# A third nested Strassen product in the attention projection, with its plain products read by ScalarE and added by GpSimd

## The chip, the cores and the metric

The kernel runs on one core of one Trainium2 chip. A core has five engines that run side by side: TensorE (PE in the profile, with its weight loads as PEld), VectorE (DVE), ScalarE (ACT), GpSimd (POOL) and SyncE (SP), which issues most of the DMAs here. The metric is the device time of one execution in microseconds (us), the median of several.

## The reference, cut to what matters

Eight images of 512 channels and 32x32 positions (1024) go through two layers. The first is self-attention with 8 heads of 64 channels:

```python
q = conv1x1(x, Wq, bq); k = conv1x1(x, Wk, bk); v = conv1x1(x, Wv, bv)   # all 512 x 512
attn = softmax(einsum('bhdn,bhdm->bhnm', q, k) * scale, axis=-1)
out = einsum('bhnm,bhdm->bhdn', attn, v)
x = x + conv1x1(out, Wp, bp)
```

The second is a non-local block: theta, phi and g are 1x1 convolutions of this x to 256 channels, f is theta times phi transposed over 1024, y is f times g, a further 1x1 convolution brings y back to 512 channels and adds x, and a batch normalisation over all images ends it. All of it is float32.

## The kernel before, in words

The images are worked off one after the other (the loop over `b`). For each image the order on TensorE is: attention of image b; q, v and k of image b+1; the projection Wp times the attention's output o of image b, called **p** (tiles `pp` and `pp_in`); theta and phi in one product (`ptp`); g (`pg`); f, wf and z. TensorE's instructions are pinned to the order in which the program gives them (`pe`), and so are all instructions marked `dve` or `sp` on the engine they run on; others may be placed by the tile framework where its own model finds the engine free. The framework makes all semaphores, and hands out buffers: a tile of a tag waits until the last reader of the tile that held that buffer is done.

**Products.** A matrix product is split into quarters 11, 12, 21 and 22 and done by Strassen's scheme in Winograd's form: seven products of sums of quarters (`SEVEN`), whose results are added up in several quarters of the output. A product's name is 11, s1t1, s2t2, s4, s3t3, 12 or t4; `s1` to `s4` are sums of weight quarters (blocks 3 to 6 of `Weights`), `t1` to `t4` sums of data quarters (`more_sums`). Each entry gives the product's name, its weight block, its data, its PSUM slot, and the quarters that it is read into, with a mark where the reading is the first (and then adds the bias).

**Nested products.** A product may itself be done by seven smaller ones (`nested`). That needs four inner sums of its weights (`inner_weights`), kept beside the block, and four of its data (`inner_sums`). For p of images 1 to 6, `FIVE` plain products (11, s1t1, s2t2, s4, s3t3) stand beside two nested ones, weight block 1 with data 21 and block 2 with t4. `INNER` holds this, and a list of counts: how many nested steps follow each plain matmul of the program. A matmul of the program is two instructions in the profile[...]. Image 0 and the last image use seven plain products.

**Slots.** PSUM is four tags of two banks each; `free` is the order in which they are to be taken. `seven` takes tags[0] and tags[1] for the slots 0 and 1 of its plain products and, with nested products, tags[2] and tags[3] for these. A later product in the same slot accumulates on what lies there, after it has been read. At its start it sets the order for the next stage, with nested products so:

```python
free[:] = [tags[1], tags[2], tags[3], tags[0]]
```

In p, slot 0 holds 11, s2t2 and s3t3 in turn, slot 1 s1t1 and s4. Theta/phi (`theta_phi`) is again a `seven` with nested products, and starts from this order.

**Reading p.** `project` reads each product from PSUM on VectorE into xt, the image's x in SBUF (line 782 with the bias, line 477 without). xt is then theta's data; its sums t1 and t2 (line 267) are made on VectorE, t4 and the inner sums of t4 and 21 on GpSimd, by `sums`, called after theta's first product.

**GpSimd's queue around p.** During v, GpSimd multiplies o by the reciprocal sums and adds v's parts. After the first third of k come the inner sums of quarter 21 of o (line 279), t1 to t4 of o (line 267) and the inner sums of t4; then `six` has it add up k: 12 += 22, 12 += T6 in its middle, 22 += T7, 21 += T7 at its end (line 402). T6 and T7 are scratch tiles of the pool `w3` (tag "acc", three buffers), which also holds theta's bias `tpb`, g and the attention's sums `acc`. Blocks of 128x1024 (`block`) come from a ring of twelve.

**Weights.** They are loaded per image, in up to three units, into four buffers (`wr`) by SP, as buffers come free (`load_w`, `fetch`); for Wp the units are blocks (1, 2), (3, 4, 5) and (6). A unit of two blocks is "roomy": it has room for inner sums. In image 0 the sums are made and the units stored in DRAM (`keep`, `keep_two`).

Of the kernel before, what the change touches and what calls it, by code (L numbers as in the profile page):

```python
# [30 lines left out]
def unshifted(ctx: ExitStack, tc: tile.TileContext, a: dict, out: bass.AP):  # L31
# [79 lines left out]
    for b in range(1, B):  # L111
# [2 lines left out]
    loaded, ahead = [], {"unit": [], "first": []}  # L114

    PAIRS = ((1, 6), (3, 4), (5, 2))
    UNITS = {"WqT": PAIRS, "WkT": PAIRS, "WvT": PAIRS, "WpT": ((1, 2), (3, 4, 5), (6,)), "tp": ((1, 2), (3, 4, 5), (6,)),
             "WgT": (range(7),)}
    WIDTH = 14 * P

# [39 lines left out]
    def fetch(w, n, t=None, dma=None):  # L160
        dma, name = dma or nc.sync, w.name
        if t is None:
            t = wf0.tile([P, 2 * w.half], F32, tag="w0", name=f"w0_{name}") if n == "first" else \
                wr.tile([P, WIDTH], F32, tag="w", name=f"w_{name}_{n}")
        blocks = w.place(n, t)
        if name in kept:
            of = kept["plain" if w.last else name][n]
            sp(dma.dma_start(w.whole(n) if w.last else w.tiles[n], of))
            return
        if n == 0:  # L170
            corner[name] = block(f"a21_{name}")[:, :, :w.half]
            sp(dma.dma_start(corner[name], quarter(name, 1, 0)))
        for i, m, k in ((0, 0, 0), (1, 0, 1), (2, 1, 1)):
            if i in blocks:
                sp(dma.dma_start(w[i], quarter(name, m, k)))
# [32 lines left out]
    def inner_weights(w, i):  # L208

        a11, a12, a22, a21, s2, s3, s4 = w.inner(i)  # L210
        return [lambda to=to, l=l, r=r, op=op: dve(nc.vector.tensor_tensor(to, l, r, op))
                for to, l, r, op in ((s3, a11, a21, ALU.subtract), (a21, a21, a22, ALU.add), (s2, a21, a11, ALU.subtract),
                                     (s4, a12, s2, ALU.subtract))]

    def nest(w, i):
        for one in inner_weights(w, i):
# [65 lines left out]
    def quarters_of(t):  # L282
# [16 lines left out]

    INNER = {"p": (FIVE, ((1, "21", "11", False), (2, "t4", "21", True)), [0] * 4 + [1] * 14),
             "tp": (FIVE, ((2, "t4", "21", True), (1, "21", "11", False)), [0] * 24 + [1] * 14)}

    def nested(name, w, data, tags, first, add, goes_to, positions_out):
# [25 lines left out]
                yield  # L331

    def seven(name, w, data, positions_out, first, add, between=None, early=False,
              by_chunk=False, inner=None):

        nk, half = w.shape[2], w.shape[3]
        tags = list(free)
        free[:] = [tags[3], tags[1], tags[0], tags[2]] if early else [tags[3], tags[1], tags[2], tags[0]]  # L340
        slots, begun = {}, set()
        steps, counts = iter(()), iter(())
        if inner:
            free[:] = [tags[1], tags[2], tags[3], tags[0]]
            products, goes_to, counts = INNER[inner]
            counts = iter(counts)
            steps = nested(name, w, data, tags[2:], first, add, goes_to, positions_out)
        else:
            products = LATER if early == "later" else EARLY if early else SEVEN

        def read(reads, ps):
            for to, is_first in reads:
                (first if is_first else add)(to, ps)

        for n, (what, wi, di, s, reads) in enumerate(products):
            if s not in slots or early and what == "t4":
                slots[s] = bank(tags[s], f"{name}_{s}_{n}")
                begun -= {one for one in begun if one[0] == s}
            ps, d = slots[s], data[di]
            if positions_out:  # L360
                parts = [(ps.rearrange("p h (i f) -> p (h i) f", f=half)[:, i, :], i * half // 512,
                          lambda k, i=i: d[:, k, i * P:(i + 1) * P], lambda k: w[:, wi, k, :])
                         for i in range(512 // P)]
            else:
                parts = [(ps[:, m, :], m, lambda k, m=m: w[:, wi, k, m * P:(m + 1) * P], lambda k: d[:, k, :])
                         for m in range(half // P)]
            work = [(*part, k) for part in parts for k in range(nk)]
            if by_chunk and what in ("11", "s1t1"):
                work.sort(key=lambda one: one[4])
            for i, (to_ps, at, lhsT, rhs, k) in enumerate(work):  # L370
                pe(nc.tensor.matmul(to_ps, lhsT(k), rhs(k), start=(s, at) not in begun, stop=(k == nk - 1),  # L371
                                    skip_group_check=True))
                begun.add((s, at))
                for _ in range(next(counts, 0)):
                    next(steps)
            read(reads, ps)
            if between and n in between:
                between[n]()

    SIX = (((1, "21", "11"), (6, "22", "12")), ((3, "t1", "22"), (4, "t2", "T6")), ((5, "t3", "T7"), (2, "t4", "21")))  # L380
    ORDER = "0a 0b 1a 2a 2b 1b 5a 4a 5b 4b 3a 3b 6a 6b".split()

    def six(name, w, data, positions_out, at, begin, third, fills, by_scalar=False):

        fills = dict(fills)
        shape = [P, 4, 256] if positions_out else [P, 2, 512]
# [75 lines left out]
        assert not fills, fills  # L462
        if by_scalar:
            add("T7", "T6")
        add("22", "T7")
        add("21", "T7")

    def rows(q):
        return q[0] if isinstance(q[0], slice) else slice((int(q[0]) - 1) * CC // 2, int(q[0]) * CC // 2)
# [65 lines left out]
    def heads_of(b, what, w, bias, data, pin=lambda ins: None, steps=None, fills=None, **how):  # L535

        t = mats.tile([P, CC, N], F32, tag=what, name=f"{what}_{b}")

        if fills is not None:
            def begin(to, ps, i):  # L540
                nc.scalar.activation(to, ps, AF.Identity, bias=bias[:, i:i + 1])

            def third(to, ps, of, i):
                if what == "q":
                    nc.scalar.activation(to, ps, AF.Identity, bias=steps[:, i:i + 1])
                else:
                    dve(nc.vector.scalar_tensor_tensor(to, ps, steps[:, i:i + 1], of, ALU.add, ALU.add))

            six(f"p{what}_{b}", w, data, False, lambda q: t[:, rows(q), cols(q)], begin, third, fills,
                what == "q")  # L550
            return t

        def first(q, ps):
            for m in range(2):
                c = rows(q).start + m
                if how.get("early") and q == "21":
                    nc.vector.tensor_scalar(t[:, c, cols(q)], ps[:, m, :], bias[:, c:c + 1], 1.0, ALU.add, ALU.mult)
                else:
                    nc.scalar.activation(t[:, c, cols(q)], ps[:, m, :], AF.Identity, bias=bias[:, c:c + 1])

        seven(f"p{what}_{b}", w, data, False, first, add_to(t, pin), **how)

        return t
# [208 lines left out]
            return o["o"], lambda ps: denominators(1, ps), lambda d: normalize((first_den, d))  # L772
        return o["o"], all_denominators, normalize

    def project(b, xt, w, between, data):
        def first(q, ps):
            if isinstance(q[0], slice):
                ps = ps.unsqueeze(1)
            for m in range(ps.shape[1]):
                c = rows(q).start + m  # L780
                at = xt[:, c, cols(q)]
                ins = nc.vector.scalar_tensor_tensor(at, ps[:, m, :], bp[:, c:c + 1], at, ALU.add, ALU.add)  # L782
                if b == B - 1 and q in ("11", "22"):
                    dve(ins)

        seven(f"pp_{b}", w, data, False, first, add_to(xt), between, early=b == B - 1 and "later",
              inner="p" if 0 < b < B - 1 else None)

# [8 lines left out]
    def theta_phi(b, w, data, tpb, between):  # L799
# [26 lines left out]
        def sums():  # L826
# [3 lines left out]
            if b:  # L830
                for of in ("t4", "21"):
                    inner_sums(data, of, dve, nc.gpsimd)

        def third_sum():
            if "t3" not in data:
# [227 lines left out]
    for b in range(B):  # L1063
        last = b == B - 1
        nxt = {}
        if b == 1:
            nest(w_tp, 1)
            nest(w_tp, 2)
            keep("tp", w_tp, (0,))
# [40 lines left out]
        if not last:  # L1110
# [13 lines left out]
            o_sums = [lambda i=i: more_sums(nxt["o"], (i,), dve, nc.gpsimd) for i in range(1, 5)]  # L1124
            if b:
                more = [lambda: inner_sums(nxt["o"], "t4", dve, nc.gpsimd)]
                o_sums = [lambda: inner_sums(nxt["o"], "21", dve, nc.gpsimd), *o_sums]
            else:
                w_p = loaded[1]
                more = [lambda i=i: weight_sums(w_p, corner["WpT"], (i,), dve, nc.gpsimd) for i in (3, 4, 5)]  # L1130
            k = heads_of(b + 1, "k", weights("WkT"), bk, data, dve, steps=dk, fills={
                (0, 13): [*o_sums, *(more if b else ())], (1, 13): () if b else more,
                (2, 0): () if b else [lambda: dve(nc.vector.tensor_tensor(bp, bp, got, ALU.add)),
                                      lambda: weight_sums(w_p, corner["WpT"], (6,), dve, nc.gpsimd)]})
        else:
            nonlocal_(b - 1, held["x"], nxt["data"], held["f"], weights("WgT"), lambda: None,
                      {4: lambda: nxt.update(d=denominators(next_bank(f"den_{b}_1")[:, 0, :]))})
# [13 lines left out]
        if not last:  # L1151
            tpb = load_tpb(b)
        w = weights("WpT", sums_done=True)
        project(b, xt, w, between, nxt["o"])
        if b == 0:
            w_p = w
        load_w("first")
# [4 lines left out]
        if b == B - LATE:  # L1162
            for cc in range(CC):
                nc.sync.dma_start(spill[b][:, cc, :], xt[:, cc, :])
        data = data_sums(quarters_of(xt), f"x1_{b}", (1, 2, 3, 4) if last else (1, 2))
        of_theta = []
        w = weights("tp")
        between = {4 if b else 5: lambda: of_theta.append(f_sums(b, tps[0], 0))}
# [268 lines left out]
```

## Time and profile before

| | us |
|---|---|
| median of 3 runs | 2102.09 (2101.91 to 2103.84) |
| the profiled execution | 2103.74 |
| its span, first to last instruction | 2102.0 |
| TensorE busy in it | 2078.5 |
| VectorE, ScalarE, GpSimd busy | 1442.3, 788.6, 734.0 |
| p of image 1, from its first weight load to theta's | 23.21 |

The span is what lies between the first and the last instruction of the profiled execution; the time of that execution is 1.7 us longer. One image is 257 us. A busy share over the whole span mixes stages: in attention VectorE and ScalarE are loaded most, around p they are not. The profile names, for idle time of an engine, the instruction that ended it. "xN" behind a row of the timeline says that N like instructions are merged in it; a row's length is that of all of them.

### The profile page before, as it was taken

The page shows a single profiled execution, that of the slowest core. Times are in us where ns is not written, and L with a number is a line of the kernel's source. Part 1 is how long each engine was busy: PE and PEld are TensorE (multiplying, and loading weights), DVE is VectorE, ACT ScalarE, POOL GpSimd, SP SyncE. Part 2 cuts the span into 40 slices and gives each one's busy share as a digit, 9 for nine tenths or more (in the row PEclk, how much of TensorE's full clock was granted, in tenths as well). Part 3 has the DMA queues.
Part 4 walks back from the last instruction along what each step waited for, and adds up shares of the span by engine and source line. Part 5 has one row for each costly group of instructions (what it writes and reads, how often), then busy time and mean ns, then how long its engine had stood idle before and what let it go on. Part 6 is the DMA issues. An engine that isn't in the chain of part 4 may idle for free.

```text
span 2102.0 us, 34269 instructions
## 1 busy us (share of the span) xinstructions
PE 2078.5 (99%) x13646; PEld 1170.3 (56%) x13646; DVE 1442.3 (69%) x2169; ACT 788.6 (38%) x1043; POOL 734.0 (35%) x637
## 2 busy tenths in 40 slices
PE   9999999999999999999999999999999999999995
PEld 4535864358733677336773377633776348743472
DVE  5587567875677656776567766677665775676756
ACT  1465203652046410464105641066312653056106
POOL 0024800348113581134812356123660338411010
PEclk9999999999999999999999999999999999999998
DMA  6254534345343443435324363253644345212668
GB/s 230 83 144 78 162 137 143 42 83 157 105 115 38 89 148 106 119 39 114 132 92 122 40 142 122 69 126 40 155 149 154 39 48 174 99 30 40 218 253 321
DMA packets 77263, 246.80 MB, mean 117 GB/s; under 512 B 17188, under 2 KB 25640, under 8 KB 75048
## 3 DMA queue, kind: packets, MB, share of 16 engines
q1 hardware_dynamic: 63224, 218.17, 31.8%
q0 software_dynamic: 12016, 24.80, 12.2%
q8 instruction: 110, 1.80, 0.4%
q10 hardware_dynamic: 1856, 1.56, 0.3%
q14 instruction: 57, 0.47, 0.1%
HBM read 163.20 MB, written 47.71 MB: 100 GB/s over the span
## 4 chain that ended last, share of the span: by engine, by line
PE 98%; ACT 1%; DVE 1%; DMA 0%; issue 0%; DVEq 0%
PE ps L611 21%; PE po L637 21%; PE pp L371 7%; PE ptp L371 7%; PE pv_in L447 6%; PE pq_in L450 6%; PE pk_in L450 6%; PE pg L371 5%; PE pz L371 3%; PE pf L866 2%; PE ptp_in_s L319 2%; PE pp_in_s L322 2%; PE pwf L909 1%; PE pv L414 1%; PE pq L417 1%; PE pq L371 1%
## 5 line engine op out<-in xcount | busy, mean ns | idle before, releaser
L614 ACT ACTIVATE e<-ps 128x1024 f32<-128x1024 f32 x512 | 522.4, 1024 | 428.7 <-PE ps L611 418.0
L667 POOL DMA_DIRECT2D fold<-acc x336 | 257.2, 816 | 949.2 <-DMA fold<-acc 450.4
L620 DVE TENSOR_TENSOR acc<-acc,e 128x1024 f32<-128x1024 f32 x384 | 469.9, 1224 | 94.5 <-ACT e L614 84.6
L611 PE MATMUL ps<-q,k 64*64 64x512 f32 x4096 | 529.3, 589 | 0.0
L637 PE MATMUL po<-e,v 64*64 64x512 f32 x4096 | 528.8, 589 | 0.0
L637 PEld LDWEIGHTS po<-e,v 64*64 64x64 f32 x4096 | 156.7, 133 | 282.8 <-issue 275.5
L611 PEld LDWEIGHTS ps<-q,k 64*64 64x64 f32 x4096 | 155.6, 133 | 283.1 <-issue 274.9
L897 ACT ACTIVATE g<-pg,gb 128x512 f32<-128x512 f32 x31 | 21.3, 687 | 447.7 <-PE pg L371 447.6
L618 DVE TENSOR_TENSOR acc<-e,e 128x1024 f32<-128x1024 f32 x64 | 78.3, 1224 | 117.6 <-ACT e L614 115.4
L371 PE MATMUL pp<-t_o,w_WpT 128*128 128x512 f32 x208 | 101.0, 592 | 0.0
L371 PE MATMUL ptp<-w_tp,t_x 128*128 128x256 f32 x400 | 96.1, 379 | 0.0
L729 POOL TENSOR_TENSOR o<-o,r 128x1024 f32<-128x1024 f32 x28 | 65.5, 2359 | 36.0 <-DMA r<-den_d 35.5
L371 PEld LDWEIGHTS ptp<-w_tp,t_x 128*128 128x128 f32 x400 | 72.3, 190 | 7.8
L458 DVE TENSOR_TENSOR k<-k,pk_in 128x256 f32<-128x256 f32 x112 | 46.8, 421 | 39.4 <-PE pk_in L450 35.0
L371 PE MATMUL ptp<-w_tp,x 128*128 128x256 f32 x272 | 69.6, 380 | 0.0
L371 PE MATMUL pp<-o,w_WpT 128*128 128x512 f32 x144 | 67.7, 592 | 0.0
L456 ACT COPY v<-pv_in 128x256 f32<-128x256 f32 x84 | 31.4, 374 | 95.8 <-DVE T_pv L458 25.5
L458 DVE TENSOR_TENSOR v<-v,pv_in 128x256 f32<-128x256 f32 x112 | 46.2, 421 | 29.3 <-PE pv_in L447 22.8
L456 ACT COPY k<-pk_in 128x256 f32<-128x256 f32 x84 | 31.2, 372 | 93.3 <-PE pk_in L450 91.6
L782 DVE SCALAR_TENSOR_TENSOR x<-pp,bp,x 128x512 f32<-128x512 f32 x52 | 37.5, 746 | 33.0 <-PE pp L371 33.0
L447 PE MATMUL pv_in<-w_WvT,i_t_x 128*128 128x128 f32 x448 | 59.2, 275 | 0.0
L450 PE MATMUL pk_in<-i_t_x,w_WkT 128*128 128x256 f32 x224 | 58.1, 381 | 0.1
(246 smaller groups left out, 3166.0 us busy)
## 6 DMA issues: line engine op xcount, KB each, us to landing
fold<-acc POOLq DMA_DIRECT2D x336, 64.0 KB, 3.0
w_WqT<-kept_WqT SPq DMA_DIRECT2D x21, 896.0 KB, 5.9
w_WvT<-kept_WvT SPq DMA_DIRECT2D x21, 896.0 KB, 5.5
w_WkT<-kept_WkT SPq DMA_DIRECT2D x21, 896.0 KB, 6.7
r<-den_d SPq DMA_DIRECT2D x32, 512.0 KB, 7.7
x<-in_x_dram SPq DMA_DIRECT2D x30, 512.0 KB, 6.0
spill<-x SPq DMA_DIRECT2D x24, 512.0 KB, 4.3
z<-spill SPq DMA_DIRECT2D x24, 512.0 KB, 8.1
```

Source lines behind the costliest of these rows:

```text
L371: pe(nc.tensor.matmul(to_ps, lhsT(k), rhs(k), start=(s, at) not in begun, stop=(k == nk - 1), skip_group_check=True))
L447: pe(nc.tensor.matmul(ps[:, i, :], d[:, i * P:(i + 1) * P], a, start=start and not i, stop=True, skip_group_check=True))
L450: pe(nc.tensor.matmul(ps, a, d, start=start, stop=True, skip_group_check=True))
L456: nc.scalar.copy(piece(q, i, j), ps)
L458: dve(nc.vector.tensor_tensor(piece(q, i, j), piece(q, i, j), ps, ALU.add))
L611: pe(nc.tensor.matmul(ps[c * P // 2:(c + 1) * P // 2, j, :], k[r, p, keys], q[r, p, h * 512:(h + 1) * 512], start=True, stop=True, skip_gr ...
L614: nc.scalar.activation(e, ps, AF.Exp, scale=SCALE)
L618: nc.vector.tensor_tensor(accs[u], es[u, 0], e, ALU.add)
L620: ins = nc.vector.tensor_tensor(accs[u], accs[u], e, ALU.add)
L637: pe(nc.tensor.matmul(ps[j * D:(j + 1) * D, r, :], v[keys, m, (2 * p + j) * D:(2 * p + j + 1) * D], e[keys, j, :], start=(m == 0), stop=(m ...
L667: nc.gpsimd.dma_start(to, of, accum_op=ALU.add)
L729: dve((engine or nc.vector).tensor_tensor(at, at, of, ALU.mult))
```

## The change

For p of images 1 to 6:

- The plain products are four (`FOUR`: 11, s1t1, s2t2, s3t3). s4, which is block 6 with data 22, becomes a third nested product, and is the first of the three: the order is block 6, block 2, block 1. A nested step follows each of the first ten plain matmuls, then 2, 1, and 2 after each of the last four.
- s3t3 stands in slot 1 and not in slot 0, in a new tile of that tag, which does not accumulate on s1t1.
- s1t1 and s2t2 are copied from PSUM by ScalarE into ring blocks (two copies of 128x512 each), and GpSimd adds the blocks to x: s1t1 into quarters 22 and 12, s2t2 into 12, 22 and, held back to the end, 21.
- s3t3 is read by VectorE at the end (`last_read`): first quarter 22 with the bias, then theta's data sums t1 and t2, then quarter 21, all pinned in this order.
- The inner sums of quarter 22 of o are added at the head of GpSimd's sums of o.
- k's last two additions (22 += T7, 21 += T7) are not made at k's end but behind GpSimd's sums for theta/phi.
- The units of Wp are (1, 2), (3, 4) and (5, 6). Block 6 with its inner sums is made once, at the start of image 1 (`nest_apart`: a load, four VectorE subtractions and a store), and loaded for each image by a DMA of its own behind block 5's.

In image 0, weight sums 5 and 6 of Wp are made on VectorE behind k, not on GpSimd within k.

```diff
-    UNITS = {... "WpT": ((1, 2), (3, 4, 5), (6,)), ...
+    UNITS = {... "WpT": ((1, 2), (3, 4), (5, 6)), ...
...
+            if n == 2 and name == "WpT" and not w.last:
+                sp(dma.dma_start(w[5], of[:, 0, :].rearrange("p (k f) -> p k f", k=2)))
+                sp(dma.dma_start(w.tiles[n][:, WIDTH // 2:], kept["block 6"]))
...
+    def nest_apart(w, n, i):
+        t = w3.tile([P, N], F32, tag="acc", name="apart")[:, :WIDTH // 2]
+        to = t[:, :2 * w.half]
+        sp(nc.sync.dma_start(to, kept["plain"][n][:, 1, :]))
+        w.at[i] = to.rearrange("p (k f) -> p k f", k=2)
+        w.extra[i] = t[:, 2 * w.half:].rearrange("p (i f) -> p i f", i=3)
+        nest(w, i)
+        kept[f"block {i}"] = dram.tile([P, WIDTH // 2], F32, tag=f"block{i}", name=f"block{i}")
+        sp(nc.sync.dma_start(kept[f"block {i}"], t))
...
-    INNER = {"p": (FIVE, ((1, "21", "11", False), (2, "t4", "21", True)), [0] * 4 + [1] * 14),
+    FOUR = (SEVEN[0], ("s1t1", 3, "t1", 1, (("22", False), ("12", False))),
+            ("s2t2", 4, "t2", 0, (("12", False), ("22", False), ("21", False))),
+            ("s3t3", 5, "t3", 1, (("22", True), ("21", False))))
+
+    INNER = {"p": (FOUR, ((6, "22", "12", True), (2, "t4", "21", True), (1, "21", "11", False)),
+                   [1] * 10 + [2, 1] + [2] * 4),
...
-            if s not in slots or early and what == "t4":
+            if s not in slots or early and what == "t4" or inner == "p" and what == "s3t3":
                 slots[s] = bank(tags[s], f"{name}_{s}_{n}")
...
-            read(reads, ps)
+            if inner and what in via:
+                via[what](reads, ps)
+            else:
+                read(reads, ps)
...
-        add("22", "T7")
-        add("21", "T7")
+        ends = [lambda q=q: add(q, "T7") for q in ("22", "21")]
+        if later is not None:
+            later += ends
+            return
+        for one in ends:
+            one()
...
+        held = []
+        def by_scalar(reads, ps):
+            t = block(f"read_{b}")
+            for m in range(2):
+                nc.scalar.copy(t[:, m, :], ps[:, m, :])
+            for n, (q, _) in enumerate(reads):
+                def one(at=xt[:, rows(q), cols(q)]):
+                    dve(nc.gpsimd.tensor_tensor(at, at, t, ALU.add))
+                if n < 2:
+                    one()
+                else:
+                    held.append(one)
+
+        def last_read(reads, ps):
+            held[0]()
+            first("22", ps)
+            more_sums(x1, (1, 2), dve)
+            add_to(xt, dve)("21", ps)
...
+            for one in data["later"]:
+                one()
...
+            nest_apart(Weights("WpT"), 2, 6)
             nest(w_tp, 1)
...
-                o_sums = [lambda: inner_sums(nxt["o"], "21", dve, nc.gpsimd), *o_sums]
+                o_sums = [*(lambda of=of: inner_sums(nxt["o"], of, dve, nc.gpsimd) for of in ("22", "21")), *o_sums]
...
+            if b == 0:
+                weight_sums(w_p, corner["WpT"], (5, 6), dve)
```

## The prediction

> **What bounds the kernel now.** First the page's busy shares and the chain of work that ended last: what holds the end?
>
> ```profile
> PE 2078.5 (99%) x13646; PEld 1170.3 (56%) x13646; DVE 1442.3 (69%) x2169; ACT 788.6 (38%) x1043; POOL 734.0 (35%) x637
> ...
> PE 98%; ACT 1%; DVE 1%; DMA 0%; issue 0%; DVEq 0%
> ```
>
> TensorE (PE) is the bound from end to end, and asked for its waits between 262 and 2050 us the profile names none. So a matmul taken out is gained in full, and a new PE wait is lost in full. Next, the p stage of image 1 in the table by stretches, from its first weight load to theta's; images 2 to 6 read 23.20 to 23.21 us too.
>
> ```profile
> core 0: us, PE busy (x) PEld busy (x) DVE busy (x) ACT busy (x) POOL busy (x), PEclk, DMA share, GB/s
> 514.17:537.38 23.21, 23.21 (x70) 13.11 (x69) 12.64 (x23) 0.37 (x1) 12.51 (x9) 1.00 0.29 99
> ```
>
> PE is full; ScalarE (ACT) is free, VectorE (DVE) and GpSimd (POOL) half busy. Third, the timeline where p hands over to theta/phi (columns: start, length, engine, line, operation, count, idle time before and its releaser):
>
> ```profile
> 533.07 1.22 DVE L477 TENSOR_TENSOR x<-x,pp 128x1024 f32<-128x1024 f32 x1 [0.44 <-PE pp L371]
> ...
> 534.53 1.22 DVE L267 TENSOR_TENSOR t_x<-x 128x1024 f32<-128x1024 f32 x1
> ...
> 535.88 1.88 PE L371 MATMUL pp<-t_o,w_WpT 128*128 128x512 f32 x4
> ...
> 537.59 3.62 PE L371 MATMUL ptp<-w_tp,x 128*128 128x256 f32 x16
> ...
> 537.79 2.35 DVE L477 TENSOR_TENSOR x<-x,pp 128x1024 f32<-128x1024 f32 x2 [1.23 <-PE pp L371]
> 540.06 1.22 DVE L267 TENSOR_TENSOR t_x<-x,t_x 128x1024 f32<-128x1024 f32 x1
> ```
>
> Theta's first matmul follows p's last without a gap although DVE reads p's last product (s3t3) until 540.1. It can: s3t3 lies in p's slot 0, while `seven` leaves `free` as [tags1, tags2, tags3, tags0], so theta's first product takes p's slot 1, whose last read (s4's, 533.07) is long over. This is the hinge of my forecast. Fourth, POOL's own timeline around p:
>
> ```profile
> 502.28 0.73 POOL L279 TENSOR_TENSOR i_o<-o 128x256 f32<-128x256 f32 x1
> ...
> 517.51 2.36 POOL L402 TENSOR_TENSOR k<-k 128x1024 f32<-128x1024 f32 x1
> 519.95 6.96 POOL L402 TENSOR_TENSOR k<-k,T_pk 128x1024 f32<-128x1024 f32 x3
> 541.42 2.35 POOL L267 TENSOR_TENSOR t_x<-x,t_x 128x1024 f32<-128x1024 f32 x1 [14.51 <-DVE t_x L267]
> ```
>
> It is solid to 526.9, then idle 14.5 us.
>
> [...] in image 0 an add of 128x4 took 2.30 us beside a POOL subtraction:
>
> ```profile
> 249.28 2.34 POOL L267 TENSOR_TENSOR t_o<-o,t_o 128x1024 f32<-128x1024 f32 x1
> ...
> 249.34 2.30 DVE L1133 TENSOR_TENSOR bp<-bp,bias 128x4 f32<-128x4 f32 x1
> ```
>
> [...] The stage tables show 1.00[...].
>
> **The change part by part** (images 1 to 6, times of image 1).
>
> *Products.* By the timeline a plain product is eight 128x512 instructions at 0.429 us (3.43 us), a nested block fourteen 128x256 ones at 0.216 (3.02). p was 5 plain and 2 nested: 17.16 + 6.05 = 23.21, as measured. It becomes 4 and 3: 13.73 + 9.07 = 22.80. Gain 0.41 us per image, 2.4 in all. First matmul at 514.38 as before, so theta could start at 537.18 instead of 537.59.
>
> *Reads moved to ACT and POOL.* Four ACT copies of 128x512 (0.58 us by ACT's copies of `po`) lie in ACT's idle time; nothing is queued behind them before `g` at 563. POOL gets four more small subtractions ("22" of o, 2.9 us) at its queue's head, so k's "12" adds end at 525.1 instead of 522.3; two k adds leave; five adds to x at 2.36 us come. s1t1 ends on PE about 524.4, its copies 525.1: x22 to 527.5, x12 to 529.9. s2t2 ends at 530.0, its copies 530.65: x12 to 533.1, x22 to 535.4, x21 to 537.75. The two nested banks are wanted at 515.2, no longer at 518.7; k's last reads leave them at 514.6 and 514.95. Data sums that p needs from POOL, shifted by 2.9, keep 1.7 us or more: t4 is ready at 517.5 for a block starting 524.3, its inner sums at 520.4.
>
> *The slot.* `FOUR` puts s3t3, now last, into slot 1, in a new tile of that tag. Theta's first product still takes p's slot 1. So it must wait until DVE has read s3t3: twice for quarter 22, and for quarter 21, which `last_read` pins behind both of theta's sums t1 and t2. DVE's chain: p's last nested matmul starts 536.97, lasts 0.38, the read adds 0.42: 537.8. Quarter 22's two halves (0.75 each) can come earlier, as x22 is ready at 535.4 and their matmuls by 536.5; they push the last nested reads to about 538.0. Before, too, such halves ran ahead of nested reads that stand earlier in the program (522.75 before 523.41). t1 needs x11 whole: 538.0. Then t1, t2 and quarter 21, 1.13 from start to start and 1.22 for the last: 541.5. A wait of 541.5 - 537.2 = **4.3 us**. If quarter 22 comes after the nested reads, 5.4. Below: were sums and reads to overlap better than rows in a queue do, 3.7. I take 4.3. Queued behind it on PE is everything, so it moves the end. Under the same cover lies a smaller new wait: nested block 1 is now last, so x11 is complete 0.5 us after theta wants it.
>
> *k's last adds.* Two times 2.36 us, behind POOL's t4, inner t4 and inner 21: with the stall 541.5 to 549.7, then to 554.4. k's lower half is read half an attention later; T7's buffer is wanted by `g` about 565 or later. Cover gone, they would cost up to 4.7 us.
>
> *Loads.* The third unit of Wp is now 256 + 448 KB in two DMAs instead of one of 256, and wanted at once, as block 6 comes first:
>
> ```profile
> 502.44 6.36 SPq L168 DMA_DIRECT2D w_WpT<-kept_plain  x2
> ...
> w_WpT<-kept_plain SPq DMA_DIRECT2D x7, 768.0 KB, 4.3
> ```
>
> The second was issued at 508.5; with one issue more (0.4) and the 4.3 us of a 768 KB load it lands near 513.3, wanted at 515.0. Nothing follows on SP's queue before 514.6. Should a load of twice the bytes take twice as long, it would cost up to 2.5 us; I take 0.
>
> *Once.* Image 1 begins with a load of 256 KB, four pinned 128x128 subtractions (0.27 each) and a store of 448 KB. The attention's sums stand behind them on DVE, with 0.5 us of slack in each step of 1.72. In the open they would cost 2.7 + 1.1 us once; I take 0. In image 0 two weight sums of 0.69 go from POOL to DVE, ahead of a DVE pause to 259.3: 0[...], still before PE needs them. DVE itself loses four half reads and whole ones worth 3.9 us per p (2 x 0.75 + 2 x 1.22) and gains seven nested reads of 0.42 (2.9): half busy as it is, that is nothing but at the hand-over.
>
> *Sum.* 6 x (4.3 - 0.41) = 23.3 us. [...] That is 25.9. The profiled execution took 2103.7 (span 2102.0 and 1.7 around it), 1.6 above the median 2102.1: 2129.6 for such a one, **2128** against the median.
>
> **The rivals.**
> - *POOL is late* (10%). POOL's five adds have about 2.4 us of slack before DVE's read of quarter 21[...]. Against it: POOL ends at 537.75, just before t1. If it is 2 to 5 us later than I count, it is added to each stall: 2140 to 2158.
> - *The bank is free in time* (13%), the other side. If theta's first product gets another bank than s3t3's, or s3t3's last read ends by 537.2 (the point that decides), only x11's lateness is left: 6 x (0.5 - 0.41), 2102.6; with that hidden too, 2099.7. For it: the hand-over before was seamless. Against it: the tags, followed in the code.
> - *Loads late* (2%): Wp's block 6 lands after 515.0 and no bank wait: 2104 to 2110.
>
> **How the numbers follow.** The bank wait has 75%; its own range, from waits of 3.7 to 5.4[...], is 2122 to 2138. I draw the range from 2119 to 2143: it leaves out the seamless case and the worst of POOL's, about 18%. About 0.2% (4.2 us) can be told from no change; the saved 2.4 us alone is below that, so the seamless case is "same" with 0.10 and faster with 0.03; slower 0.87.
>
> **What would show it.** Right: in images 1 to 6 PE idle 4 to 5.5 us before `ptp`, released by DVE's last read of `pp`, after two `t_x`; p itself 22.8 us. Wrong: no gap there; or a gap released by a POOL add of x; or gaps inside p at a nested block. The forecast fails if the bank of theta's first product is not s3t3's.

## The result, and the profile after

| | before | after |
|---|---|---|
| median of 6 runs, us | 2102.74 | 2150.43 (2148.20 to 2150.76) |
| span of the profiled execution, us | 2102.0 | 2149.0 |

The ratio is 1.0224, with an interval from 1.0211 to 1.0237: the kernel is slower by some 48 us. The forecast was 2128, slower, with a range that ended at 2143. The sign and the wait for the bank came out as told. The length of that wait, and the slow clock behind it, did not.

The page of the kernel after, its busy times and the chain that ended last:

```profile
PE 2092.6 (97%) x13682; PEld 1186.3 (55%) x13682; DVE 1452.7 (68%) x2193; ACT 802.1 (37%) x1067; POOL 814.8 (38%) x689
...
PE 95%; DVE 3%; ACT 1%; issue 0%; DMA 0%; DVEq 0%
```

TensorE is still the bound, but VectorE's share of the chain grew from 1% to 3%. And TensorE's busy time grew by 14.1 us (2078.5 to 2092.6), though the change takes work from it. Both have to be explained. First, what TensorE waited for between 262 and 2090 us, where before no wait was named (us in all, times, longest):

```profile
PE ptp L391 <- DVE x L504: 32.1, 6, 5.4
PE ptp_in_s L339 <- DVE tp L865: 0.7, 2, 0.5
```

Six waits, one per image 1 to 6, of theta's first product for VectorE's read of p's last. (Lines 391, 504, 282, 342, 809 and 425 are 371, 477, 267, 322, 782 and 402 of before, moved down by the new code.) The table by stretches, p of image 1 from its first weight load to theta's, which answers to the 23.21 us of before:

```profile
core 0: us, PE busy (x) PEld busy (x) DVE busy (x) ACT busy (x) POOL busy (x), PEclk, DMA share, GB/s
514.98:543.32 28.34, 23.19 (x76) 14.06 (x74) 15.73 (x29) 2.52 (x5) 22.36 (x13) 1.00 0.37 121
```

TensorE's timeline in this hand-over (start, length, engine, line, operation, count, idle time before and its releaser):

```profile
536.29 1.02 PE L391 MATMUL pp<-t_o,w_WpT 128*128 128x512 f32 x2
537.14 0.59 PE L342 MATMUL pp_in_s<-o,w_WpT 128*128 128x256 f32 x2
537.58 0.59 PE L342 MATMUL pp_in_s<-i_o,w_WpT 128*128 128x256 f32 x2
543.53 5.20 PE L391 MATMUL ptp<-w_tp,x 128*128 128x256 f32 x16 [5.36 <-DVE x L504]
```

p itself runs without a gap to the nested matmul at 537.58; theta starts at 543.53. There are two losses here. One is the hole. The other is the length of the last row: before, the same 16 matmuls took 3.62 us, now 5.20. VectorE in the same stretch:

```profile
537.78 0.85 DVE L504 TENSOR_TENSOR x<-x,pp_in_s 128x256 f32<-128x256 f32 x2 [0.87 <-PE pp_in_s L342]
538.55 1.40 DVE L809 SCALAR_TENSOR_TENSOR x<-pp,bp,x 128x512 f32<-128x512 f32 x2
539.87 1.22 DVE L282 TENSOR_TENSOR t_x<-x 128x1024 f32<-128x1024 f32 x1
541.12 1.22 DVE L282 TENSOR_TENSOR t_x<-x,t_x 128x1024 f32<-128x1024 f32 x1
542.26 1.21 DVE L504 TENSOR_TENSOR x<-x,pp 128x1024 f32<-128x1024 f32 x1
```

This is the order of the program: the last two nested reads, both halves of quarter 22, t1, t2, then quarter 21, whose end at 543.47 frees the bank. Nothing in it waits for GpSimd, whose adds to x end before quarter 21 is wanted:

```profile
526.45 4.67 POOL L821 TENSOR_TENSOR x<-x,read 128x1024 f32<-128x1024 f32 x2 [0.51 <-ACT read L818]
532.11 6.97 POOL L821 TENSOR_TENSOR x<-x,read 128x1024 f32<-128x1024 f32 x3 [0.99 <-ACT read L818]
```

The second loss is the clock. Stretches of 3 us behind the hole of image 1 and of image 2 (two answers' rows together; the granted clock is the third value from the end):

```profile
543.50:546.50 3.00, 2.97 (x7) 2.44 (x8) 0.00 (x0) 0.00 (x0) 2.81 (x2) 0.50 0.00 0
546.50:549.50 3.00, 3.00 (x15) 2.63 (x15) 0.73 (x1) 0.00 (x0) 2.92 (x5) 0.99 0.00 0
807.50:810.50 3.00, 2.97 (x7) 2.43 (x8) 0.00 (x0) 0.00 (x0) 2.80 (x2) 0.50 0.04 15
810.50:813.50 3.00, 3.00 (x10) 2.38 (x10) 0.00 (x0) 0.00 (x0) 2.92 (x5) 0.62 0.00 0
```

At half clock TensorE did 7 instructions in 3 us, at full clock 15. The record of the clock over the whole execution shows 0.5 behind all six holes: for 3.41 us in images 1 and 4, for 6.83 us in 2, 3, 5 and 6, and nowhere else between the start and the end. A wait does not count as busy; work at half clock does. That is, for the most part, how TensorE's busy time grew.

By the starts of the stages in the two traces, for images 1 to 6 together, against the spans' difference of 47.0 us:

| | us |
|---|---|
| p's own work, 22.80 for 23.21 | -2.5 |
| the hole before theta, 5.52 each | +33.1 |
| theta/phi, 23.57 to between 25.16 and 26.68: its plain part, half clock | +14.2 |
| theta/phi: its nested part, short waits for VectorE's reads of theta/phi | +1.5 |
| other stages, the start and the end | +0.7 |

The second and third rows differ in kind, and so the experiments have to tell them apart: is the bank the cause of the hole, and is the hole the cause of the slow theta?

### The profile page after: what moved, and what is told of

Same layout as the page of the kernel before. It is cut to its first block, busy times and chain, and to the rows that moved or that the text cites. A ratio compares the mean times of both kernels' runs of the same rounds, so it can differ in the third digit from the quotient of the medians.

```text
span 2149.0 us, 34474 instructions
## 1 busy us (share of the span) xinstructions
PE 2092.6 (97%) x13682; PEld 1186.3 (55%) x13682; DVE 1452.7 (68%) x2193; ACT 802.1 (37%) x1067; POOL 814.8 (38%) x689
## 4 chain that ended last, share of the span: by engine, by line
PE 95%; DVE 3%; ACT 1%; issue 0%; DMA 0%; DVEq 0%
PE ps L638 21%; PE po L664 20%; PE ptp L391 7%; PE pv_in L470 6%; PE pp L391 6%; PE pq_in L473 6%; PE pk_in L473 6%; PE pg L391 4%; PE pz L391 3%; PE pp_in_s L342 2%; PE pf L916 2%; PE ptp_in_s L339 2%; PE pwf L959 1%; PE pv L437 1%; PE pq L440 1%; PE pq L391 1%
## 5 line engine op out<-in xcount | busy, mean ns | idle before, releaser
L391 PE MATMUL ptp<-w_tp,x 128*128 128x256 f32 x272 | 83.8, 441 | 32.1 <-DVE x L504 32.1
L391 PEld LDWEIGHTS ptp<-w_tp,x 128*128 128x128 f32 x272 | 57.2, 227 | 43.4 <-DVE x L504 34.5
L821 POOL TENSOR_TENSOR x<-x,read 128x1024 f32<-128x1024 f32 x30 | 69.8, 2353 | 10.7 <-ACT read L818 10.7
L865 DVE TENSOR_TENSOR tp<-ptp,tpb 128x1024 f32<-128x1024 f32 x25 | 30.5, 1221 | 55.7 <-PE ptp L391 55.7
```

The source lines that it names most:

```text
L821: dve(nc.gpsimd.tensor_tensor(at, at, t, ALU.add))
```

## The experiments

The kernel before, run beside them, took 2103.27 us in the first group (e1 to e4) and 2102.97 in the second. Edits are against the kernel after, or against e5 where said.

### e1: another bank for theta's first product

After p, theta's first product is sent to tags[0], whose last product was s2t2, and p's slot 1 is handed out last. Nothing else moves.

```diff
-            free[:] = [tags[1], tags[2], tags[3], tags[0]]
+            free[:] = [tags[0], tags[2], tags[3], tags[1]] if inner == "p" else [tags[1], tags[2], tags[3], tags[0]]
```

> The changed kernel with one line different: after p of images 1 to 6 the tags are handed on as [tags0, tags2, tags3, tags1], so that theta's first product takes the bank that ScalarE emptied (s2t2's) and not the one that holds s3t3. Order and number of all instructions stay. Theory A (the wait is for s3t3's bank, and the cold clock follows from that wait): the 5.4 us wait per image shrinks to about 0.6 (x11's last nested read), no half clock inside the kernel, all of 2150.4 - 2102.7 comes back: about 2103 (2102.7 - 6 x 0.41 + 6 x 0.6 = 2103.9). Theory B (GpSimd's adds to x are late and hold theta up): the wait stays near 5 us and the time near 2145 to 2150. Theory C (x11, completed by the last nested block, is what theta waits for): the wait stays as well.

Measured: 2102.61 us, ratio 0.9998 (0.9990 to 1.0006), span 2101.9. One line takes back the whole loss. TensorE at the hand-over of e1:

```profile
537.04 0.59 PE L342 MATMUL pp_in_s<-i_o,w_WpT 128*128 128x256 f32 x2
537.76 3.69 PE L391 MATMUL ptp<-w_tp,x 128*128 128x256 f32 x16
```

and VectorE there:

```profile
537.24 0.85 DVE L504 TENSOR_TENSOR x<-x,pp_in_s 128x256 f32<-128x256 f32 x2 [0.87 <-PE pp_in_s L342]
538.01 1.40 DVE L809 SCALAR_TENSOR_TENSOR x<-pp,bp,x 128x512 f32<-128x512 f32 x2
539.33 1.22 DVE L282 TENSOR_TENSOR t_x<-x 128x1024 f32<-128x1024 f32 x1
540.58 1.23 DVE L282 TENSOR_TENSOR t_x<-x,t_x 128x1024 f32<-128x1024 f32 x1
541.73 1.22 DVE L504 TENSOR_TENSOR x<-x,pp 128x1024 f32<-128x1024 f32 x1
```

VectorE is exactly as late: its five rows follow each other in the same order and distances as in the kernel after, and quarter 21 is read at 541.7, 4 us into theta. Now nobody waits for it. So the lateness of the read costs nothing by itself; the bank that it holds does. The clock stayed at 1.00 behind p in all six images (the run's mean is 0.996, as in the kernel before; in the kernel after it is 0.988), and theta/phi took 23.65 us. What is left of p's gain is small: p with its gap is 23.09 us, of which 0.29 is a wait for x11, since the nested block that fills quarter 11 now comes last; e5 below, where that block is done earlier, has no such wait.

### e2: quarter 21 read ahead of the sums

The read that frees the bank goes ahead of t1 and t2.

```diff
             first("22", ps)
-            more_sums(x1, (1, 2), dve)
             add_to(xt, dve)("21", ps)
+            more_sums(x1, (1, 2), dve)
```

> The changed kernel with the read of quarter 21 of s3t3 put ahead of theta's sums t1 and t2. Theory A: the bank is free 2.3 us sooner, so the wait per image falls from 5.4 to about 3.2 us; t1 and t2 follow at about 2 and 3 us after that, before theta needs them. [...] the time is about 2102.7 - 2.4 + 6 x 3.2 = 2119.5; [...] up to 6 x 1.7 to 6 x 3.4 us more: 2130 to 2140. Theory C: the wait is unchanged, 2150.

Measured: 2126.59 us, ratio 1.0111 (1.0095 to 1.0126), span 2124.5. The waits of TensorE in e2:

```profile
PE ptp L391 <- DVE x L504: 17.8, 6, 3.0
```

Two sums fewer in the chain shorten the wait from 5.36 to 2.96 us (the hole, from the end of the last nested matmul's step, from 5.52 to 3.12): 2.40 for two rows that stand 1.14 to 1.25 apart. The chain is read rightly, row by row. The time lies between the two that were expected, 2119.5 with the clock at full and 2130 or more with it halved, since only some of the holes were followed by half clock.

e2 also tells more of the clock, because its holes are all alike and what followed was not. Theta/phi lost 1.55, 1.79 and 0.11 us in images 1 to 3, then 1.79, 0.11 and 1.71. Behind the hole of image 1, and the hole of image 3 with what follows it:

```profile
539.70:542.70 3.00, 3.00 (x7) 2.46 (x8) 2.31 (x2) 0.00 (x0) 0.52 (x1) 0.51 0.30 127
...
1060.10:1063.10 3.00, 0.04 (x2) 0.02 (x1) 2.99 (x6) 0.00 (x0) 0.92 (x1) 1.00 0.83 259
1063.10:1066.10 3.00, 3.00 (x14) 2.67 (x15) 2.29 (x2) 0.00 (x0) 0.54 (x1) 1.00 0.35 131
```

Image 3 had the same hole (0.04 us busy in 3 us), and TensorE came back at full clock: 14 instructions in 3 us, where image 1 had 7. By the losses of theta/phi, half clock followed the hole of 3.12 us in four images of six. What set these four apart was not shown.

### e3: the wait filled with work

Six matmuls of 128x512 (twelve instructions) stand between p and theta, in the bank that comes last in the order. Both their operands are data that are there; their results are not read. The wait stays as it is, TensorE is busy through it.

```diff
+        if 0 < b < B - 1:
+            fill = bank(free[3], f"fill_{b}")
+            of = data["t1"]
+            for i in range(6):
+                pe(nc.tensor.matmul(fill[:, i % 2, :], of[:, 0, :P], of[:, 0, :], start=True, stop=True, ...))
```

> The changed kernel with six added matmuls of 128x512 (twelve instructions, 5.15 us) between p and theta in images 1 to 6, into a bank that lies free, on data that is there; their results are never read. Nothing else waits for them and the wait for s3t3's bank is as long as they last. It tells the cold clock from the wait. Theory A: the wait of 5.4 to 5.7 us stays as busy time, but the clock stays at 1.00 and theta/phi takes 23.6 us again and not 25.2 to 26.8: about 2150.4 - 15.7 + 1 = 2135.5. If the slower theta/phi stage has another cause than the idle wait: 2150 or more.

Measured: 2138.68 us, ratio 1.0168 (1.0152 to 1.0183), span 2137.7. TensorE at the hand-over of e3:

```profile
537.47 5.31 PE L840 MATMUL fill<-t_o 128*128 128x512 f32 x12
542.99 3.72 PE L391 MATMUL ptp<-w_tp,x 128*128 128x256 f32 x16 [0.21 <-DVE x L504]
```

From p's last matmul to theta's first there are 5.52 us, as in the kernel after, and theta's first 16 matmuls take 3.72 us and not 5.20; the clock is 1.00 up to 2119 us (0.996 in the run's mean, as in the kernel before). So some 12 us of the loss went with the clock alone (2150.43 less 2138.68 is 11.75; each taken against the kernel before beside it, 12.3). That is less than the 14.2 of the table, for this reason, in TensorE's waits of e3:

```profile
PE ptp_in_s L339 <- DVE tp L871: 2.8, 6, 0.5
PE ptp L391 <- DVE x L504: 1.2, 6, 0.2
```

At full clock theta's nested matmuls catch up with VectorE's late reads of theta/phi and wait for them, about 0.71 us per image with the shorter waits, 4.2 in all, where the kernel after had 1.5 in all; these 2.7 us lie under the slow matmuls of the kernel after.

### e4 and e5: can the gain of the third nested product be had?

Both have e1's bank, and end p with a plain matmul, so that the last nested block is done earlier. e4:

```diff
-                   [1] * 10 + [2, 1] + [2] * 4),
+                   [1] * 10 + [2, 2, 2, 3, 2, 0]),
```

> As the run with the other bank, and the nested steps of p placed earlier: the counts end 2, 2, 2, 3, 2, 0 and not 2, 1, 2, 2, 2, 2, so that nested block 1 is done before the last plain matmul and x11 is complete when theta starts. Theory A with C as its smaller part: the 0.6 us per image that x11 costs in the run with the other bank is gone, at up to 0.2 us for three nested steps in a row: about 2101 to 2102, that is 2 to 3 us below that run and 1 to 2 below the kernel before (2102.7 - 2.4 = 2100.3 at best). If x11 costs nothing there: the same as that run.

Measured: 2103.24 us, ratio 1.0000 (0.9991 to 1.0008). Theta starts without a gap, but p takes 23.15 us: a wait of 0.24 us appeared inside p, at the place with three nested steps in a row: the third starts at 533.71, where VectorE's read of an earlier one ends at 533.66. The wait was moved, not removed, and the 1 to 2 us that were expected below the kernel before did not come. e5 has no more than two in a row:

```diff
-                   [1] * 10 + [2, 1] + [2] * 4),
+                   [1] * 9 + [2] * 6 + [0]),
```

> As the run with the other bank, with counts of nine 1, six 2 and one 0: the nested steps never come three in a row (three in a row cost 0.24 us per image in the run with bank and counts), and x11 is still complete before theta. By theory A nothing is left to wait for: p takes 22.8 us and theta/phi 23.57 in images 1 to 6, as against 23.21 and 23.57 before, that is 2.4 us less in all: 2103.3 - 2.4 = 2100.9, a ratio of 0.9988. If the added reads by ScalarE and GpSimd, the loads or the clock cost something that the bank's wait hid, it is 2102 or more.

Measured: 2101.07 us (2100.23 to 2102.04), ratio 0.9992 (0.9983 to 1.0000), span 2099.3. p is 22.80 us and theta/phi 23.57 in all six images, so 6 x 0.41 = 2.5 us are gained by the stages, and 1.9 by the medians. That is under what can be told from no change, though the interval's end is at 1. It is the best of the kernels run. TensorE in e5 at the hand-over:

```profile
535.80 1.02 PE L391 MATMUL pp<-t_o,w_WpT 128*128 128x512 f32 x2
536.66 3.62 PE L391 MATMUL ptp<-w_tp,x 128*128 128x256 f32 x16
```

e6 and e7 start from e5, where the bank hides nothing, and undo one of the two other parts each.

### e6: k's last additions back at k's end

```diff
-            k = heads_of(b + 1, "k", weights("WkT"), bk, data, dve, steps=dk, later=later, fills={
+            k = heads_of(b + 1, "k", weights("WkT"), bk, data, dve, steps=dk, fills={
```

> As the run with the other bank and paired steps, but k's last two additions stay at k's end, ahead of GpSimd's adds to x. It measures what GpSimd's lateness costs (theory B), with the bank's wait out of the way. GpSimd then ends its five adds 4.7 us later; quarter 22 is read by VectorE only about 2 us after p's end[...]: theta's second product would wait 2 to 3 us per image. Expected 2101 + 6 x 2.5 = 2116, up to 2126 if the clock falls in these gaps too. If GpSimd has more room than I count: 2101.

Measured: 2110.83 us, ratio 1.0035 (1.0022 to 1.0049), span 2111.1: 9.8 us more than e5, where 15 were expected. GpSimd in e6, then VectorE in e6:

```profile
522.41 6.96 POOL L425 TENSOR_TENSOR k<-k,T_pk 128x1024 f32<-128x1024 f32 x3
529.33 11.74 POOL L821 TENSOR_TENSOR x<-x,read 128x1024 f32<-128x1024 f32 x5
```

```profile
538.78 1.41 DVE L809 SCALAR_TENSOR_TENSOR x<-pp,bp,x 128x512 f32<-128x512 f32 x2 [1.86 <-POOL x L821]
540.11 2.04 DVE L282 TENSOR_TENSOR t_x<-x 128x1024 f32<-128x1024 f32 x1
542.18 1.22 DVE L282 TENSOR_TENSOR t_x<-x,t_x 128x1024 f32<-128x1024 f32 x1
```

GpSimd's five adds now run without a pause to 541.07. VectorE waits 1.86 us for them, and t1, which begins 0.96 us before GpSimd's last add ends, takes 2.04 us, where it takes 1.22 in the kernel after and in e1. p stays at 22.80; theta/phi loses 0.7 to 4.2 us, with half clock in image 4. This edit brings about the rival "POOL is late": the wait of 1.86 us and the 0.82 us more of t1 are there, but the change itself keeps clear of both by putting k's additions off.

e6 also tells of the clock. TensorE's hole in theta is 2.23 us long in image 4 and 2.35 us in image 6, yet only the shorter one was followed by half clock. The stretch that holds most of the hole and the one behind it, for image 4 and then image 6:

```profile
1315.54:1318.95 3.41, 1.18 (x6) 1.06 (x6) 3.38 (x4) 0.00 (x0) 1.07 (x1) 1.00 0.41 142
1318.95:1322.36 3.41, 3.41 (x9) 2.69 (x8) 2.27 (x3) 0.00 (x0) 2.13 (x1) 0.50 0.00 0
...
1820.71:1824.12 3.41, 1.48 (x7) 0.95 (x5) 3.03 (x3) 0.00 (x0) 2.65 (x2) 1.00 0.73 274
1824.12:1827.54 3.42, 3.00 (x14) 2.69 (x15) 3.39 (x4) 0.00 (x0) 0.56 (x1) 1.00 0.06 23
```

In image 4 TensorE is busy for 1.18 of 3.41 us, and then works at 0.50: 9 instructions in 3.41 us. In image 6 it is busy for 1.48 of 3.41 us and 3.00 of the next 3.42, idle for 2.35 in all, and the clock stays at 1.00. So the length of a hole alone does not tell whether half clock follows; what else decides was not shown.

### e7: VectorE reads s1t1 and s2t2 itself

```diff
-            held[0]()
+            for one in held:
+                one()
...
-              via={"s1t1": by_scalar, "s2t2": by_scalar, "s3t3": last_read})
+              via={"s3t3": last_read})
```

> As the run with the other bank and paired steps, but s1t1 and s2t2 are read by VectorE straight into the quarters (five adds of 1.22 us each per image) and nothing by ScalarE and GpSimd. It tells what the detour is worth. VectorE is then busy some 17 of p's 23 us; long reads stand between the short nested ones, so that single nested steps may wait. Expected: within 2 us of the run that it is made from if VectorE has room (2101 to 2103), up to 1 us more per image (2107) where nested steps wait for a read.

Measured: 2112.86 us, ratio 1.0047 (1.0031 to 1.0062), span 2110.6. VectorE, then TensorE, in e7:

```profile
532.18 2.35 DVE L504 TENSOR_TENSOR x<-x,pp 128x1024 f32<-128x1024 f32 x2
```

```profile
534.92 0.70 PE L342 MATMUL pp_in_s<-o,w_WpT 128*128 128x256 f32 x2 [0.93 <-DVE x L504]
```

p takes 24.74 us, 1.94 more than in e5: two whole reads, 2.35 us together, hold VectorE while nested products wait in their banks to be read, and TensorE waits for a bank; the 0.93 us of this row are its longest wait of several. Six times 1.94 is 11.6; the medians differ by 11.8. At most 1 us per image had been expected.

So the parts of the change hang together. With three nested products the detour through ScalarE and GpSimd and the putting off of k's additions are worth 11.8 and 9.8 us. What cost 48 us is that theta's first product was sent to the bank that is read last: changing that order alone takes it back.

## Why the prediction was right or wrong

**The slot: right.** The hinge, that theta's first product takes p's slot 1 and s3t3 now lies there, decided the case: e1 changes only that and ends within 0.1% of before. The releaser is the one named, behind two sums, in all six images.

**p's own work: right.** 22.80 us against 23.21, as worked out, and had in full in e5.

**The wait, 4.3 us: too short by 1.2.** It measured 5.52. The step that failed is "Quarter 22's two halves can come earlier, as x22 is ready at 535.4 and their matmuls by 536.5". The matmuls were on time: the product ends at 537.31, which is 536.5 and the 0.83 us by which p starts later. But 538.0 for x11 needs the first half ahead of the product's end, and the halves came behind both nested reads. Two things held them. First, a half did not come when its own matmuls were done: it waited for the whole product. In e5 the first of these rows ends the first half's matmuls, at 533.38, and x22 is there by 535.9; VectorE stands idle from 536.42, and takes both halves, in one row, only when s3t3 has ended at 536.82 (535.80 and 1.02):

```profile
532.36 1.02 PE L391 MATMUL pp<-t_o,w_WpT 128*128 128x512 f32 x2
...
536.93 1.41 DVE L809 SCALAR_TENSOR_TENSOR x<-pp,bp,x 128x512 f32<-128x512 f32 x2 [0.51 <-PE pp L391]
```

The precedent that I took from the kernel before, the half at 522.75, had done the same: its product ended at 522.71. Whether the framework's semaphores or the chip ask for this, no run tells. Second, VectorE kept the order of the program, in which the last two nested reads stand ahead of the halves: in the kernel after it is idle until 537.78, 0.47 us past the product's end, and begins the halves at 538.55. By these rows the order alone is worth some 0.4 us, an estimate: halves at 537.42 and nested reads behind them would have let t1 start at about 539.5, and it started at 539.87. The wait for the whole product is most of the rest. My bound for that case, "If quarter 22 comes after the nested reads, 5.4", was the right sum; I chose the wrong end. Six times 1.22 is 7.3 us.

**The clock, 0.4 us per image: the larger miss.** The 0.4 us, 2.6 in all, were my estimate; no trace from before the change showed a slow clock behind a hole, since p had no hole there. I had put a slow stretch at a quarter of the cases. Measured: half clock in six of six images, 14.2 us instead of 2.6, 2.4 us each. Two things in the step failed. Half clock was not the exception: it followed each of the six holes of 5.52 us. And the slow stretch lasted 3.41 us only in images 1 and 4; in the four others it was 6.83. With the wait at 4.3 us, as I had it, four images of six or more would still have been slow: an estimate from e2, where that many were slow behind holes of 3.12 us. In e6 half clock came even behind a hole of 2.23 us.

The sum: 21.1 us of span lie between the forecast's working (2102.0 + 25.9, which is 23.3 and those 2.6) and 2149.0: 7.3 from the wait, 11.6 from the clock, 1.5 from theta's nested waits, 0.7 from other stages. The range took one end of each term, but gave the clock no more than 1 us per image; with 5.5 and 2.4 it would have read 2147.

**POOL is late: refuted for the change, brought about in e6.** GpSimd ended at 539.08 where I had 537.75 (1.33 late, of which 0.83 is a later start of p), and VectorE needed it at 542.3. t1 and t2 took 1.22 us each. e6 shows what it would have cost.

**The bank is free in time: refuted,** and its price borne out: e1 gives 2102.61 where that rival had 2102.6 with x11's lateness left (0.29 us before theta and 0.08 in it, where 0.5 was told, so the agreement to 0.01 us is in part luck), e5 2101.07 where it had 2099.7 with that hidden too.

**Costed at nothing: right.** The loads of Wp's blocks brought no wait inside p in any image. k's last additions ran from 551.8 to 557.4 with nobody waiting. What is done once does not show: the stages ahead of image 1's p moved by 0.83 us together, 0.77 of it in the first q of image 0.

## What to carry to other kernels

When a product is given another place in PSUM, write down the order in which the banks of the stage become free by their last *read*, and compare it with the order in which the next stage takes them; the bank read last has to be taken last, and then a late read is free, as in e1, where it came 4 us into theta. A hole in TensorE's work is to be priced with the slow clock behind it, here 2.4 us on top of 5.5, and shorter holes are not safe from it: half clock followed all six holes of 5.52 us in the kernel after, four of the six of 3.12 us in e2, and in e6 one of 2.23 us but not one of 2.35. Where a bundle of edits loses, undo the smallest one first: two parts of this one were worth about 10 us each, and a single order of four tags hid that.

## What the runs showed of the hardware

- At a granted clock of 0.50 TensorE did 7 instructions of theta in 3 us, at 0.99 it did 15 (kernel after, image 1). The first 16 matmuls of theta took 5.20 us there, 3.62 in the kernel before and 3.72 in e3.
- The slow stretches behind the six holes of the kernel after lasted 3.41 us (images 1 and 4) or 6.83 us (2, 3, 5 and 6). Half clock followed six of six holes of 5.52 us there, four of six of 3.12 us in e2, and in e6 a hole of 2.23 us but not one of 2.35 us. What decides is not shown; no run was made to find it. Idle time is taken from the ends of matmuls that the profile models.
- A VectorE sum (t1) took 2.04 us in e6, where it began 0.96 us before the end of a GpSimd add; in the kernel after, where GpSimd's adds had ended 0.79 us before it, it took 1.22.
- Filling the wait with matmuls whose results nobody reads made the kernel some 12 us faster (e3, 2138.68 us against 2150.43): behind this wait an idle TensorE cost more than a busy one.
